# Two accumulator tiles in the second pass: which block of a unit lies in which one

## The chip, the cores and the metric

The kernel runs on one core of a Trainium2 chip. The metric is the device time of one execution in microseconds (us), lower is better; the median of a few runs is compared. One further execution was taken with the hardware profiler, and all rows below come from that one.

The engines are named as in the profile: PE is the matrix engine and PEld its weight loads, ACT the scalar engine, DVE the vector engine, POOL the general one, SP the one that issues most DMAs.

## The reference, cut to what matters

Two layers work on an image batch `x` of 8 x 96 x 96 pixels with 192 channels, float32 throughout. Layer 0 normalizes `x` by groups, projects it to 384 channels, convolves it 3 x 3, adds four running averages, normalizes each pixel over its 384 channels and projects back to 192. Layer 1 normalizes by groups, convolves 7 x 7, and has a two-layer network with a gelu per pixel. The change is in the part that ends layer 0:

```python
mu = jnp.mean(mixed, axis=-1, keepdims=True)
var = jnp.mean(jnp.square(mixed - mu), axis=-1, keepdims=True)
normed = (mixed - mu) * jax.lax.rsqrt(var + LN_EPS) * ln_g + ln_b
return jnp.einsum('bhwc,cd->bhwd', normed, W_out) + b_out   # then x + ...
```

## The kernel before, in words

The program is written in passes, one after the other, each with its own pools of buffers. The first pass (lines 245 to 570) is the group norm and the projection to 384 channels; it keeps its result in DRAM. The next (lines 605 to 827) is the 3 x 3 convolution with the running averages, and leaves `mixed` in DRAM as `M_d`, channels along the partitions. The pass of this change follows (lines 1045 to 1293; the change's own words call it the second pass). Last come the 7 x 7 convolution (`conv_d`, matmuls on line 1337) and the two-layer network (lines 1534 to 1595). Inside the pass the order on each engine is the order of the code: it stands under `manual_schedule`, and an engine's list of instructions is worked off strictly from the front.

**Units and blocks.** The pass goes over 192 units (`n_u`). A unit is one image column of four images, 384 pixels, and it has three blocks `j` of 128 pixels. For each block:

- `turn_c` (line 1135) transposes the 384 channels of the 128 pixels into a tile `pt`, three PE instructions.
- `project_c` (line 1141) multiplies the same pixels by the output weights `wc` and accumulates over three channel chunks `m` into a slot `po` of 193 columns. A float32 product is two PE instructions, so there are six. The last column of `wc` is 1/384, so column 193 of the slot is the pixel's mean.
- `square_c` (lines 1160 and 1162) runs on ACT: it copies the mean out of `po[:, D:]`, and then takes the sum of squares of `pt - mean` into column `j` of `var`.

One unit later, in this order: `scale_c` (lines 1168 and 1170) makes `rs` from `var`, first on DVE and then as a power on POOL; `finish_c` (line 1175) has DVE read the three slots `po`, j = 0, 1, 2 in turn, scale them by `rs`, add the input `xr` and write `x1c`. On DVE three statistics of `x1c` (line 1192) stand between the two in most units. On POOL the addition of a constant to the next `xr` (line 1261) follows the power.

**The accumulators.** `tile_po` takes two tiles of two slots each from a pool of four tiles (`ps_o`), each tile in a PSUM bank of its own. Three of the four slots are used. So the two tiles of a unit are handed out again two units later, and the first matmul into one of them then waits until `finish_c` has read all that lay in it. Waits are set by tile: a matmul into one slot of a tile also waits for an engine that still reads the other slot. `pt` has a pool of three tiles (`ps_t`), one a block.

**Loads and stores.** In the iteration of unit u, SP issues the loads of unit u+3 (`mt` in two parts of 384 and 192 KB, line 1111, and `xr` of 288 KB, line 1123), and, when a group of 16 units is complete, one of its twelve stores of 384 KB each (line 1211) in each of the next twelve units. `mt` has four buffers. In the last 36 units loads for the next pass are added (`raw` on line 926, on SP and POOL, and `band` on line 936). After unit 95 the group norm's sums over the first half are made, in five steps, one a unit (`norm_c`, lines 988 to 1043): DVE waits in them for small matmuls of PE.

**The start.** Because `M_d`'s last rows come late, the first two chunks (`range(NC - 1)`) of some blocks of units 0 and 1 are multiplied ahead of the loop (lines 1231 to 1233). `ms` on line 1265 says, for these two units, which chunks are left to each block.

Of the kernel before, what the change touches and what calls it, by code (L numbers as in the profile page):

```python
# [101 lines left out]
def conv_blocks_kernel(  # L102
# [36 lines left out]
    NC = C // 128  # L139
# [111 lines left out]
    with ExitStack() as ph:  # L251
# [258 lines left out]
        with tc.manual_schedule():  # L510
# [13 lines left out]
            for b in range(B):  # L524
                more = b + 1 < B
                for t in range(n_t):
                    u = b * n_t + t

                    n, j = divmod(u - 2, NJ)
# [25 lines left out]
                    k, j = divmod(t, NJ)  # L555
# [489 lines left out]
    with ExitStack() as ph:  # L1045
# [10 lines left out]
        NJ3 = 3  # L1056
# [4 lines left out]
        def make_wc(stores):  # L1061
            ps = ps_s.tile([128, 512], F32, tag="gn_ps", name="ps_w")
            nc.gpsimd.memset(wc[:, :, D:], 1.0 / C)
            for m in range(NC):
                nc.scalar.activation(
                    wc[:, m, :D], wo[:, m], AF.Identity, scale=gb[:, 0, m : m + 1]
                )
            for step in stores:
                step()
            for lo, lhs, rhs in ((D, lnb, wo), (0, None, wc)):  # L1070
                for m in range(NC):
                    nc.tensor.matmul(
                        ps[:, lo : lo + D],
                        mean_w if lhs is None else lhs[:, m],
                        rhs[:, m, :D],
                        start=(m == 0),
                        stop=(m == NC - 1),
                    )
            for m in range(NC):
                nc.vector.tensor_tensor(wc[:, m, :D], wc[:, m, :D], ps[:, :D], ALU.subtract)  # L1080
            nc.vector.tensor_tensor(cst, bo, ps[:, D : 2 * D], ALU.add)
            nc.gpsimd.memset(blk, 0.0)
            for b in range(NH):
                q = slice(b * QH, (b + 1) * QH)
                nc.gpsimd.memset(blk[q, q], 1.0 / QH)
                nc.gpsimd.tensor_copy(
                    pick[:, b], ident[:, b * QH : b * QH + 1].to_broadcast([128, 128])
                )
# [13 lines left out]
        def load_m(u, k):  # L1102

            hf, p, v = place_c(u)
            w = v * PH + p
            if u not in mts and u < 3:
                mts[u] = first[:, u].rearrange("p (m n) -> p m n", m=NC)
            elif u not in mts:
                mts[u] = ip.tile([128, NC, NH * S], F32, tag="mt", name="mt")
            m = (slice(0, CS // 128), slice(CS // 128, NC))[k]  # L1110
            nc.sync.dma_start(
                mts[u][:, m],
                M_f[k][S - 1 - w, :, hf * NH * S : (hf + 1) * NH * S].rearrange(
                    "(m c) n -> c m n", c=128
                ),
            )

        def load_x(u):

            hf, p, v = place_c(u)  # L1120
            w = v * PH + p
            xrs[u] = ip.tile([128, NJ3, D], F32, tag="xr", name="xr", bufs=5)
            nc.sync.dma_start(
                xrs[u],
                x_f[hf * NH * S : (hf + 1) * NH * S, w].rearrange("(i j) c -> i j c", j=NJ3),
            )

        def load_c(u):
            for k in range(2):
                load_m(u, k)  # L1130
            load_x(u)

        def turn_c(mt, pt, j, ms):
            for m in ms:
                nc.tensor.transpose(
                    pt[:, m * 128 : (m + 1) * 128], mt[:, m, j * 128 : (j + 1) * 128], ident
                )

        def project_c(mt, po, j, ms):
            for m in ms:  # L1140
                nc.tensor.matmul(  # L1141
                    po,
                    mt[:, m, j * 128 : (j + 1) * 128],
                    wc[:, m],
                    start=(m == 0),
                    stop=(m == NC - 1),
                )

        def tile_pt():
            return ps_t.tile([128, C], F32, tag="pt", name="pt")  # L1150

        def tile_po():
            pa = ps_o.tile([128, 2, D + 1], F32, tag="po", name="po")
            pb = ps_o.tile([128, 2, D + 1], F32, tag="po", name="po")
            return [pa[:, 0], pa[:, 1], pb[:, 0]]

        def square_c(pt, po, var, j):

# [60 lines left out]
        with tc.manual_schedule():  # L1219
            for u in range(3):  # L1220
                load_m(u, 0)
            make_wc(late_b)
            for u in range(3):
                load_m(u, 1)
            for u in range(3):
                load_x(u)
            pos_c = {u: tile_po() for u in range(2)}
            pts_c = {j: tile_pt() for j in range(NJ3)}
            for j in range(NJ3):
                turn_c(mts[0], pts_c[j], j, range(NC - 1))  # L1230
            for u in range(2):
                for j in range(0, NJ3, 2):
                    project_c(mts[u], pos_c[u][j], j, range(NC - 1))
            weights = load_weights()
            for u in range(n_u + 1):
                if weights and u >= 8:
                    with nc.allow_non_contiguous_dma(reason="one value per partition"):
                        nc.scalar.dma_start(*weights.pop(0))
                if u + 3 < n_u:
                    load_c(u + 3)  # L1240
                if stores:
                    stores.pop(0)()
                if u == n_u - 36:
                    early_d = [lambda: load_band(0)]
                    early_d += [lambda t=t: load_raw(0, t) for t in range(NT)]
                    early_d += [lambda: load_band(1)]
                if u >= n_u - 36 and u % 3 == 0 and early_d:
                    early_d.pop(0)()
                if u == n_u - 14:
                    first_d += scale_steps(0)  # L1250
                    for t in range(NT):
                        first_d.insert((t + 1) * 9 - 1, lambda t=t: load_raw(1, t))
                if u >= n_u - 14:
                    for step in first_d[:3]:
                        step()
                    del first_d[:3]
                if held is not None:
                    rs = scale_c(held[1])
                if u < n_u:
                    mt, xr = mts.pop(u), xrs.pop(u)  # L1260
                    nc.gpsimd.tensor_tensor(
                        xr, xr, cst.unsqueeze(1).to_broadcast([128, NJ3, D]), ALU.add
                    )
                    var = sp.tile([128, NJ3], F32, tag="var", name="var")
                    ms = [range(NC - 1 if u in pos_c and j != 1 else 0, NC) for j in range(NJ3)]
                    pos = pos_c.pop(u) if u in pos_c else tile_po()
                    for j in range(NJ3):
                        pt = pts_c.pop(j) if j in pts_c else tile_pt()
                        turn_c(mt, pt, j, range(0 if u else NC - 1, NC))
                        project_c(mt, pos[j], j, ms[j])  # L1270
                        square_c(pt, pos[j], var, j)
                if steps:
                    for step in steps.pop(0):
                        step()
                if held is not None:
                    n, v = divmod(u - 1, WQ)
                    if v == 0:
                        x1c = xps[1 - n % 2].tile([128, NJ3, D, WQ], F32, tag="x1c", name="x1c")
                    finish_c(x1c, v, held[0], rs, held[2])
                    if v == WQ - 1:  # L1280
                        steps += group_steps(x1c, n)
                        stores += [
                            lambda x=x1c, n=n, j=j, q=q: store_c(x, n, j, q)
                            for j in range(NJ3)
                            for q in range(NX)
                        ]
                held = (pos, var, xr) if u < n_u else None
            for step in first_d:
                step()
            for store in stores:  # L1290
                store()
            for step in sum(steps, []):
                step()

    WE = 8
    NJ3 = 3
# [487 lines left out]
```

## Time and profile before

| What | us |
|---|---|
| median of 3 runs (5494.1 to 5501.23) | 5495.28 |
| the profiled execution's own time | 5491.53 |
| its span, first to last instruction | 5489.7 |
| the pass of the change, from the span's start | 1803 to 2621 |
| PE busy over the span | 5298.0 (97%) |
| L1141, the pass's projections, on PE: 3456 instructions | 686.7 |
| L1135, its transposes, on PE: 1728 instructions | 283 |

How to read it: the time of an execution is some 2 us longer than its span. A row of the timeline gives start, duration, engine, line, operation, the tiles written and read, and the count; the brackets at the end give the idle time of the engine just before, and who ended it. Rows of PEld are the weight loads that go ahead of each matmul and run beside the one before.

### The profile page before, as it was taken

The numbers are of one execution on the slowest core, as the hardware profiler recorded it, in microseconds if no ns is written. First come the engines' busy times: TensorE is split into PE (matmuls) and PEld (weight loads), VectorE is DVE, ScalarE is ACT, GpSimd is POOL, SyncE is SP. The second block draws the span as 40 slices with busy tenths as digits, with TensorE's granted clock in tenths as the row PEclk, the third lists the DMA queues.
The fourth block names the chain that finished last, engine by engine and source line by source line (L and its number), as shares of the span: only waits on it lengthen the run. The fifth ranks groups of instructions, "written<-read, shape, count | busy, mean of one in ns | idle before, by whom it ended". The sixth has DMA issues, their size and how long they took to land. (4 is left out here: it accounts for less than half of the span.)

```text
span 5489.7 us, 108072 instructions
## 1 busy us (share of the span) xinstructions
PE 5298.0 (97%) x42206; PEld 3359.4 (61%) x42206; DVE 3450.2 (63%) x6706; ACT 2593.6 (47%) x5781; POOL 2366.2 (43%) x2063
## 2 busy tenths in 40 slices
PE   6999999999999999999787899999999999999999
PEld 4666643333333899899454566666666676666767
DVE  6556539999999455555556455555566666656654
ACT  2444447777777566566434444444433233333332
POOL 1211128888888555555322232322233333333332
PEclk9999979999999999999898999999999999999999
DMA  7999869999998899899996454555433233333231
GB/s 222 285 288 276 245 179 244 243 243 244 246 242 230 247 293 293 260 287 315 290 294 171 117 136 124 131 137 137 111 90 80 79 79 80 88 91 84 79 79 41
DMA packets 793486, 1015.35 MB, mean 185 GB/s; under 512 B 331191, under 2 KB 668320, under 8 KB 790928
## 3 DMA queue, kind: packets, MB, share of 16 engines
q1 hardware_dynamic: 677000, 634.43, 44.2%
q0 software_dynamic: 84304, 331.93, 18.2%
q10 hardware_dynamic: 31672, 42.08, 3.4%
q8 instruction: 333, 5.46, 0.4%
q14 instruction: 177, 1.45, 0.1%
HBM read 603.70 MB, written 420.03 MB: 186 GB/s over the span
## 5 line engine op out<-in xcount | busy, mean ns | idle before, releaser
L1574 PEld LDWEIGHTS hp<-w1g,g 128*128 128x128 f32 x6912 | 1117.9, 190 | 140.7 <-issue 75.8
L1574 PE MATMUL hp<-w1g,g 128*128 128x192 f32 x6912 | 1174.9, 329 | 0.0
L1563 ACT ACTIVATE g<-hp,b0g 128x512 f32<-128x512 f32 x864 | 520.2, 693 | 1211.3 <-PE hp L1554 1188.0
L1593 POOL DMA_DIRECT2D out_dram<-xo x288 | 211.6, 735 | 1574.4 <-DVE xo L1585 1480.7
L1585 DVE TENSOR_TENSOR xo<-hp,r 128x384 f32<-128x384 f32 x288 | 229.0, 795 | 992.9 <-PE hp L1574 987.9
L1544 PE MATMUL hp<-yT,w0w 128*128 128x512 f32 x1728 | 780.6, 598 | 20.3 <-DVE yT L1529 20.3
L1141 PE MATMUL po<-wc,mt 128*128 128x193 f32 x3456 | 686.7, 334 | 7.4 <-DVE x1c L1175 7.1
L688 PE MATMUL pl<-pin,band 34*32 34x380 f32 (+1 forms) x13824 | 640.2, 497 | 6.2 <-DMA pin<-PL_d 4.0
L775 POOL TENSOR_TENSOR mo<-mo,z 128x768 f32<-128x768 f32 x285 | 592.5, 2079 | 5.7 <-ACT mo L713 1.6
L1141 PEld LDWEIGHTS po<-wc,mt 128*128 128x128 f32 x3456 | 555.7, 191 | 39.4 <-ACT mean L1160 31.0
L1544 PEld LDWEIGHTS hp<-yT,w0w 128*128 128x128 f32 x1728 | 321.5, 191 | 380.9 <-issue 346.2
L721 DVE TENSOR_TENSOR_SCAN z<-decay,loc 128x768 f32<-128x768 f32 x288 | 506.0, 1757 | 64.7 <-ACT loc L697 36.3
L1337 PE MATMUL hp<-xin,band 63*64 63x372 f32 (+1 forms) x4608 | 422.8, 503 | 95.2 <-ACT yo L1347 35.6
L730 DVE TENSOR_TENSOR_SCAN z<-decay,z 128x768 f32<-128x768 f32 x288 | 498.5, 1731 | 0.1
L688 PEld LDWEIGHTS pl<-pin,band 34*32 34x32 f32 x13824 | 234.1, 108 | 394.1 <-issue 390.1
L1508 POOL TENSOR_TENSOR rs<-tot,neg_half 32x32 f32<-32x32 f32 x72 | 394.8, 5483 | 122.3 <-DVE tot L1506 121.0
L709 PE MATMUL pa<-loc,mix 128*32 128x384 f32 x3456 | 439.4, 500 | 0.0
L712 PE MATMUL pa<-last,down 96*32 96x384 f32 x1152 | 434.2, 500 | 1.0 <-ACT mo L713 1.0
L1554 PE MATMUL hp<-yT,w0w 64*128 64x512 f32 x1728 | 419.5, 611 | 0.0
L1347 ACT ACTIVATE yo<-hp,dwb 128x384 f32<-128x384 f32 x384 | 197.6, 585 | 435.6 <-PE hp L1337 272.8
L697 ACT COPY loc<-pl 128x384 f32<-128x384 f32 x576 | 248.6, 484 | 312.7 <-PE pl L688 312.7
L395 PE MATMUL pm<-xT,win 128*128 128x384 f32 x1152 | 391.7, 490 | 0.0
(155 smaller groups left out, 7248.1 us busy)
## 6 DMA issues: line engine op xcount, KB each, us to landing
P<-po POOLq DMA_DIRECT2D x96, 1152.0 KB, 9.5
pin<-P SPq DMA_DIRECT2D x190, 576.0 KB
mt<-M SPq DMA_DIRECT2D x192, 384.0 KB
xq<-in_x_dram SPq DMA_DIRECT2D x96, 576.0 KB
xr<-in_x_dram SPq DMA_DIRECT2D x192, 288.0 KB
X<-x1c SPq DMA_DIRECT2D x144, 384.0 KB
out_dram<-xo POOLq DMA_DIRECT2D x288, 192.0 KB, 2.5
r<-X SPq DMA_DIRECT2D x35, 1536.0 KB
```

The source lines that it names most:

```text
L688: nc.tensor.matmul(pls[g][at * RB : (at + 1) * RB, :, lo:hi], band[rows, c, kh, :], pin[rows, c, :, NJ - 1 - j, lo + kh - 1 : hi + kh - 1] ...
L709: nc.tensor.matmul(pa[at], mix[:, i, at], loc[:, q], start=True, stop=True)
L712: nc.tensor.matmul(pa[at], down[:, to], last[:, q], start=True, stop=True)
L721: nc.vector.tensor_tensor_scan(zf, decay_f, loc.rearrange("p q n -> p (q n)"), 0.0, ALU.mult, ALU.add)
L730: nc.vector.tensor_tensor_scan(zr, decay_f, zr, 0.0, ALU.mult, ALU.add)
L775: eng.tensor_tensor(m, m, z, ALU.add)
L1141: nc.tensor.matmul(po, mt[:, m, j * 128 : (j + 1) * 128], wc[:, m], start=(m == 0), stop=(m == NC - 1),)
L1337: nc.tensor.matmul(pys[g][k * 64 : (k + 1) * 64, :, lo:hi], band[rows, k * GS + c, d * ZS : d * ZS + 64], xin[rows, :, :, k * GS + c, lo + ...
L1544: nc.tensor.matmul(hps[m, q], w0w[:, 0, m * 128 : (m + 1) * 128], yT[:, 2 * q], start=True, stop=False,)
L1554: nc.tensor.matmul(hps[m, q], w0w[p, 1, m * 128 : (m + 1) * 128], yT[p, 1], start=False, stop=True,)
L1563: nc.scalar.activation(g[:, m, q], hps[m, q], AF.Gelu, bias=b0g[:, m : m + 1], scale=1.0)
L1574: nc.tensor.matmul(po[:, q], g[:, m, q, k * 128 : (k + 1) * 128], w1g[:, m], start=(m == 0), stop=(m == NE - 1),)
```

## The change

The second and the third block of a unit change slots: block 1 goes to the first slot of the second tile, and block 2 to the second slot of the first tile. What is multiplied ahead of the loop changes with it: blocks 0 and 1 of the first two units in place of blocks 0 and 2.

```diff
-            return [pa[:, 0], pa[:, 1], pb[:, 0]]
+            return [pa[:, 0], pb[:, 0], pa[:, 1]]
...
             for u in range(2):
-                for j in range(0, NJ3, 2):
+                for j in range(2):
                     project_c(mts[u], pos_c[u][j], j, range(NC - 1))
...
-                    ms = [range(NC - 1 if u in pos_c and j != 1 else 0, NC) for j in range(NJ3)]
+                    ms = [range(NC - 1 if u in pos_c and j < 2 else 0, NC) for j in range(NJ3)]
```

In the order of instructions, TensorE's list alone differs, in some ten rows of units 0 and 1; the number of instructions is the same on every engine. The waits differ: block 1's first projection waits for DVE as block 0's does, block 2's for ACT, and the first transpose of block 2 has two things to wait for (PE and ACT) where it had one (PE).

## The prediction

> **What bounds the kernel now.** I read the page first: PE is busy 97% of the span, so only what PE waits for in the pass of the change can be won. Of the page's groups these two are the projections of that pass. The columns after the bar are busy us, mean ns, and PE's idle time just before with who ended it.
>
> ```profile
> span 5489.7 us, 108072 instructions
> ...
> L1141 PE MATMUL po<-wc,mt 128*128 128x193 f32 x3456 | 686.7, 334 | 7.4 <-DVE x1c L1175 7.1
> ...
> L1141 PEld LDWEIGHTS po<-wc,mt 128*128 128x128 f32 x3456 | 555.7, 191 | 39.4 <-ACT mean L1160 31.0
> ```
>
> The matmuls themselves hardly wait (7.4 us), but their weight loads stood still 31.0 us for ACT's copy of the mean. Busy matmuls hide this: a PE row that began without its weights ready is only longer. The waits inside 1804 to 2621 give the count (total us, times, longest):
>
> ```profile
> PEld po L1141 <- ACT mean L1160: 31.0, 190, 0.5
> ...
> PEld pt L1135 <- DMA mt<-M: 8.5, 4, 7.9
> PEld po L1141 <- DVE x1c L1175: 8.1, 4, 3.6
> ```
>
> So once a unit, in 190 of 192 units. The timeline of one steady unit shows what such a wait costs. Block 0 begins at 2102.64, block 1 at 2103.95, block 2 at 2105.45, the next unit at 2106.77:
>
> ```profile
> 2102.64 0.49 PE L1135 MATMUL pt<-ident,mt 128*128 128x128 f32 x3
> ...
> 2102.97 1.15 PE L1141 MATMUL po<-wc,mt 128*128 128x193 f32 x6
> ...
> 2103.95 0.49 PE L1135 MATMUL pt<-ident,mt 128*128 128x128 f32 x3
> ...
> 2104.15 0.16 ACT L1160 COPY mean<-po 128x1 f32<-128x1 f32 x1 [0.45 <-PE po L1141]
> ...
> 2104.36 0.95 PEld L1141 LDWEIGHTS po<-wc,mt 128*128 128x128 f32 x6 [0.16 <-ACT mean L1160]
> 2104.36 1.25 PE L1141 MATMUL po<-wc,mt 128*128 128x193 f32 x6
> ...
> 2104.95 1.28 DVE L1175 SCALAR_TENSOR_TENSOR x1c<-po,rs,xr 128x192 f32<-128x192 f32 x3
> 2105.29 0.41 PEld L1135 LDWEIGHTS pt<-ident,mt 128*128 128x128 f32 x3
> 2105.45 0.49 PE L1135 MATMUL pt<-ident,mt 128*128 128x128 f32 x3
> ...
> 2106.77 0.49 PE L1135 MATMUL pt<-ident,mt 128*128 128x128 f32 x3
> ```
>
> ACT's copy of block 0's mean (2104.15, 0.16 long) ends at 2104.31, and block 1's projection, into the same tile, begins 0.05 later. Blocks 0 and 2 project 0.33 after their transposes, block 1 only 0.41 after; and its six matmuls take 1.25 and not 1.15, as no weights were ready. From start to start the blocks take 1.314, 1.501 and 1.314 (medians over 189 or 190 units): a wait costs **0.187 us**, and a unit 4.13.
>
> **The change part by part.**
>
> *The wait that goes.* Block 1 now writes the second tile, so it need not wait for ACT to read block 0's mean. Block 2 does instead (it shares the first tile with block 0), but it projects one block, over 1.3 us, after that copy ended; nothing is late there. The three blocks should all take 1.314: 190 x 0.187 = **-35.5 us**. If hidden weight loads alone were won it would be the 31.0 of the waits view; I take the spacing, which counts PE itself.
>
> *An added wait instruction.* Block 2's transposes now have two things to wait for. Such pairs stand in the trace as a separate 51 ns instruction of PE's sequencer, two a unit (382), ahead of blocks 0 and 1. Block 2 has none. The step from block 2 to block 0, which has one, is 1.314 like the one without: nothing, as the sequencer runs ahead of PE. Bounds 0 and 190 x 0.051 = 9.7; I take 0.
>
> *A later release.* Block 0 of unit u+2 takes the first tile again. That tile was free after `finish_c`'s reads of blocks 0 and 1; now it needs those of 0 and 2, the last of the three, some 0.4 later (1.28 for three). Behind this wait stands all of PE's list. In the unit shown the three reads end at 2106.23, and the weight load they must precede is at 2106.99. Over all units that gap is 0.73 to 0.75 at nearly every one; with a unit 0.187 shorter and 0.05 for the signal, **0.50 us is left**. So it costs nothing in the steady part. Where `norm_c` holds DVE up, it does:
>
> ```profile
> 2270.89 1.26 DVE L1175 SCALAR_TENSOR_TENSOR x1c<-po,rs,xr 128x192 f32<-128x192 f32 x3
> 2271.84 2.20 PE L1141 MATMUL po<-wc,mt 128*128 128x193 f32 x6 [3.32 <-DVE x1c L1175]
> ```
>
> PE starts 0.32 before the last of the three reads ends; now it will start 0.05 after. Four units are like this: 4 x 0.37 = **+1.5 us**.
>
> *What is late next: the DMAs.* A unit with a store moves 384 + 192 + 288 + 384 KB = 1.278 MB, 309 GB/s at 4.13 us; twelve of sixteen units have one, the others move 0.885 MB. At 3.94 us it is 324 GB/s in those twelve. To see the room, I counted the 1536-byte packets off against the issues of `mt`: up to unit 158 they are in 5 to 9 us ahead of their first transpose (least 2.6, at unit 64), of the three units' lead (12.4). Should the DMAs give no more than today's 309, twelve units lose 12 x 0.187 = 2.2 us of that room, and the four without a store give it back. So it is hidden. In the last 36 units it isn't (columns: us, busy of PE, PEld, DVE, ACT, POOL, clock, DMA share, GB/s):
>
> ```profile
> 1900.00:2000.00 100.00, 100.00 (x656) 94.47 (x655) 53.28 (x148) 60.41 (x218) 54.05 (x48) 1.00 0.95 298
> ...
> 2500.00:2540.00 40.00, 40.00 (x262) 37.55 (x261) 23.73 (x66) 24.04 (x88) 23.12 (x21) 1.00 1.08 335
> ...
> 2570.00:2612.00 42.00, 41.35 (x267) 38.30 (x265) 28.25 (x80) 24.83 (x90) 24.24 (x23) 1.00 1.08 310
> ```
>
> With the loads for the next pass the DMAs are full, and the room falls from 6.7 at unit 159 to 0.21 at unit 172, rises to 8.7 at 179, and falls to 0.13 at unit 190, after PE had already waited 1.1 us in two blocks (one row: 0.47 for `mt` at 2603.15). If the DMAs are no faster, a shorter unit takes 0.56 (three units' lead) and 0.187 a unit from this. At unit 172: 0.21 - 0.56 - 13 x 0.187 = -2.8. At unit 190: 0.13 - 1.1 - 0.56 - 8 x 0.187 = -3.0, of which 1.1 is paid today. So **+2.8 and +1.9, together +4.7 us**. Bounds: 0 (the DMAs can give more), and the whole gain of these 36 units, 6.7.
> The Trainium skill weighs on this: its page "DMA: Bandwidth & Descriptors", in "Where 436 GB/s comes from", gives some 358 GB/s as one core's share of the memory. By it the 335 above had room left, the tail would cost nothing, and the time would be some 5 us lower. The rows of the trace, a share of 1.08 with the room shrinking, speak against it.
>
> *The start.* Four pairs of chunks are multiplied ahead of the loop as before, only for other blocks. PE waits there for `mt` (7.6 and 7.9 us), so this costs nothing, with 0.3 either way.
>
> *What follows.* The next pass begins with `finish_c` of the last unit: the last twelve stores go out from 2623.47, behind them on SP's queue the next `band`, and PE waits 21.2 us for that. All of it hangs on the end of this pass and moves with it. Between 2621 and 3070 the clock flips often, which may add or take a few us.
>
> **Sum:** -35.5 + 1.5 + 4.7 = -29.3. The profiled execution would go from 5491.53 to 5462.2; the median shown is 3.75 above it, so 5495.28 - 29.3 = **5466**.
>
> **The rivals.**
>
> *The DMAs bind all through the pass.* Then the units with a store stay at 4.13 and only four of sixteen gain: 35.5 / 4 = 9 us, 5486. For it: a share of 0.95 already. Against: 5 us of room and 335 GB/s where asked for. Chance 0.08.
>
> *The time of block 1 isn't the wait's.* If PE needs the 0.187 for changing tiles, nothing moves: 5495. Against: blocks 0 and 2 also change tiles (block 2 to the second, block 0 to the next unit's) without it. Chance 0.03.
>
> *Slower: the later release becomes the bound.* From the last projection of a unit (ends 2102.80) over ACT, `ve`, `rs` and three reads to the release (2106.28) takes 3.48 us, and there is one unit for it, 3.94. It decides from 3.94 on, and beyond 4.13 the pass is slower than now: `rs` on POOL (0.86) or a statistic on DVE would have to take 0.65 more. The 0.42 of one read, paid in each of 190 units, is 80 us against 35.5: 5540. Against: the gap is the same to 0.02 us in nearly all units. Chance 0.03.
>
> *The clock.* After the 3.32 us stall above PE ran at half clock (2.20 for six matmuls in place of 1.25), which cost 1.7 us in the rows that follow. If the two DMA stalls of the tail and one longer stall of `norm_c` do that, and some of the flips after 2621 fall badly, it is 5 to 9 us: 5473. Chance 0.06.
> The Trainium skill's "TensorE: Matmul & The Clock Gate", under "A second HAM failure mode: psum-queue depth-cycling", tells of small idle times from cycling through PSUM banks that drop the clock over and over. The trace doesn't bear that out: four tiles are cycled through here now, at a granted clock of 1.00.
>
> **How the numbers follow.** The forecast has 0.80. A change under 0.2%, 11 us, can't be told from none. Faster: 0.80 + 0.06 + half of the first rival 0.04 = 0.90; same: 0.04 + 0.03 = 0.07; slower 0.03. The range's low end is -35.5 with no cost of `norm_c` or tail and 3 us for the runs' spread: 5457. Its high end takes in 9.7 for the wait instruction, or the clock with a dearer tail: 5481. What is left out is most of the first rival, no effect, and slower.
>
> **What would show it.** Right: no wait of L1141's weight loads for ACT's mean, blocks of 1.31 all three, a steady unit of 3.94, mean PE time of L1141 near 329 ns; the four waits for `x1c` longer by 0.4 each; waits for `mt` of about 3 us near units 172 and 190, and the next pass some 29 us earlier. Wrong: waits for `x1c` in many units, a third wait row in each unit with a gap behind it, or units of 4.1 with waits for `mt`.

## The result, and the profile after

The changed kernel took 5463.48 us (median of 6 runs, 5442.51 to 5470.07), the kernel before 5494.4 beside it (6 runs, 5479.02 to 5501.23): a ratio of **0.995**, interval 0.9933 to 0.9967. On a second chip it was 5464.61 (10 runs) against 5487.31 (15 runs), ratio 0.9957 (0.9943 to 0.9971). 5466 was forecast. The profiled execution took 5470.07 us, its span is 5468.3, so it is 21.4 shorter in span than that of before.

The page after, the two groups of the pass's projections:

```profile
L1141 PE MATMUL po<-wc,mt 128*128 128x193 f32 x3456 | 668.8, 329 | 7.4 <-DVE x1c L1175 7.3
...
L1141 PEld LDWEIGHTS po<-wc,mt 128*128 128x128 f32 x3456 | 557.7, 192 | 9.0 <-DVE x1c L1175 8.6
```

The weight loads' wait for ACT's mean is gone from its place in the second row (39.4 us of idle time before, 9.0 now), and the matmuls, though as many, are 17.9 us less busy: those of the second block are no longer stretched. The timeline of a steady unit after, from block 0 to block 0:

```profile
2100.45 0.49 PE L1135 MATMUL pt<-ident,mt 128*128 128x128 f32 x3
...
2101.77 0.49 PE L1135 MATMUL pt<-ident,mt 128*128 128x128 f32 x3
2101.97 0.16 ACT L1160 COPY mean<-po 128x1 f32<-128x1 f32 x1 [0.45 <-PE po L1141]
2101.99 0.96 PEld L1141 LDWEIGHTS po<-wc,mt 128*128 128x128 f32 x6
2102.09 1.15 PE L1141 MATMUL po<-wc,mt 128*128 128x193 f32 x6
...
2103.08 0.49 PE L1135 MATMUL pt<-ident,mt 128*128 128x128 f32 x3
...
2104.39 0.49 PE L1135 MATMUL pt<-ident,mt 128*128 128x128 f32 x3
```

The blocks are 1.31 apart throughout. ACT copies a mean from 2101.97 to 2102.13, and PE's next projection begins within that time, at 2102.09; before, it stood 0.05 behind the copy's end.

The gain did not last to the end of the pass. These are PE's waits for `mt` from 2400 to the pass's end (total us, times, longest), first after, then before:

```profile
PE pt L1135 <- DMA mt<-M: 7.5, 7, 3.6
```

```profile
PE pt L1135 <- DMA mt<-M: 0.5, 1, 0.5
```

So I split the pass by the first transposes of its units in each trace, for all kernels (us; the last column is from the pass's first transpose to the first matmul of the 7 x 7 convolution):

| Kernel | steady unit | units 2-109 | 109-115 (`norm_c`) | 115-159 | 159-191 (extra loads) | whole pass |
|---|---|---|---|---|---|---|
| before | 4.131 | 442.1 | 37.1 | 181.7 | 133.9 | 817.4 |
| changed | 3.944 | 422.3 | 36.6 | 173.5 | 138.6 | 792.9 |
| changed, second profile | 3.944 | 422.3 | 36.5 | 173.5 | 136.9 | 791.1 |
| changed, loads moved | 3.944 | 422.0 | 34.9 | 175.6 | 127.0 | 781.7 |
| before, loads moved | 4.129 | 441.8 | 35.6 | 182.3 | 132.1 | 814.9 |
| blocks 1 and 2 share | 4.130 | 441.9 | 35.7 | 181.7 | 135.9 | 818.8 |
| a tile for each block | 5.302 | 567.7 | 42.5 | 233.3 | 169.8 | 1039.0 |
| changed, block 1 read first | 3.944 | 422.3 | 33.8 | 173.5 | 135.8 | 787.5 |
| both: loads moved, block 1 first | 3.944 | 421.9 | 33.8 | 175.0 | 127.7 | 780.1 |

In the profiled executions the pass gained 24.5 us. Another 2.3 had been gained before it began, and 5.4 were lost after it, where nothing was changed. Most of these were lost in the first 380 us behind the pass, where the mean granted clock was 0.86 and not the 0.87 of before; what brought that about is open. The column 109-115 holds a difference that was in no kernel's plan: behind its waits the granted clock fell to half for 3.4 us, twice in the first three rows, and once only in the rows with the loads moved or block 1 read first. One such stretch is worth some 1.6 us there.

### The profile page after: what moved, and what is told of

Read it like the earlier page. It is cut to its first block, busy times and chain, and to the rows that moved or that the text cites. A ratio compares the mean times of both kernels' runs of the same rounds, so it can differ in the third digit from the quotient of the medians.

```text
span 5468.3 us, 108263 instructions
## 1 busy us (share of the span) xinstructions
PE 5262.7 (96%) x42206; PEld 3344.9 (61%) x42206; DVE 3451.2 (63%) x6706; ACT 2588.0 (47%) x5781; POOL 2364.3 (43%) x2063
## 5 line engine op out<-in xcount | busy, mean ns | idle before, releaser
L1544 PE MATMUL hp<-yT,w0w 128*128 128x512 f32 x1728 | 780.1, 597 | 20.8 <-DVE yT L1529 20.8
L1141 PE MATMUL po<-wc,mt 128*128 128x193 f32 x3456 | 668.8, 329 | 7.4 <-DVE x1c L1175 7.3
L1337 PE MATMUL hp<-xin,band 63*64 63x372 f32 (+1 forms) x4608 | 423.3, 504 | 100.0 <-ACT yo L1347 39.4
```

What stands on the lines that cost most here:

```text
L1141: nc.tensor.matmul(po, mt[:, m, j * 128 : (j + 1) * 128], wc[:, m], start=(m == 0), stop=(m == NC - 1),)
L1337: nc.tensor.matmul(pys[g][k * 64 : (k + 1) * 64, :, lo:hi], band[rows, k * GS + c, d * ZS : d * ZS + 64], xin[rows, :, :, k * GS + c, lo + ...
L1544: nc.tensor.matmul(hps[m, q], w0w[:, 0, m * 128 : (m + 1) * 128], yT[:, 2 * q], start=True, stop=False,)
```

## The experiments

Theory: the wait for ACT's copy cost 0.187 us a unit, it is gone, and from unit 159 on the DMAs take back what a shorter unit wins. Rivals: block 1 was slow for another reason (its slot, a change of tile); the late release of the first tile, or the clock, is what slows the tail.

**Blocks 1 and 2 share.** Block 0 has the first tile alone:

```diff
-            return [pa[:, 0], pb[:, 0], pa[:, 1]]
+            return [pa[:, 0], pb[:, 0], pb[:, 1]]
```

> Block 0 alone in the first tile, blocks 1 and 2 in the two slots of the second. Theory: the wait for ACT's copy of the mean comes back, now in front of block 2 (for block 1's mean), 190 times, blocks of 1.31, 1.31 and 1.50, a unit of 4.13, the time that of before within 3 us (5490 to 5497). The first tile is free after one read, so the stalls where the group norm holds DVE up get 0.4 shorter each. Rival (block 1 was slow for lying in the second slot or for the change of tile, not for the wait): no long block, or another one than block 2, and 5463.

Measured: 5491.2 us (10 runs) against 5487.88 for the kernel before on the same chip, ratio 1.0011 (1.0001 to 1.0021). The timeline of blocks 1 and 2 of one unit:

```profile
2106.16 0.49 PE L1135 MATMUL pt<-ident,mt 128*128 128x128 f32 x3
...
2106.49 1.15 PE L1141 MATMUL po<-wc,mt 128*128 128x193 f32 x6
...
2107.48 0.49 PE L1135 MATMUL pt<-ident,mt 128*128 128x128 f32 x3
...
2107.89 0.95 PEld L1141 LDWEIGHTS po<-wc,mt 128*128 128x128 f32 x6 [0.16 <-ACT mean L1160]
2107.89 1.25 PE L1141 MATMUL po<-wc,mt 128*128 128x193 f32 x6
...
2108.98 0.49 PE L1135 MATMUL pt<-ident,mt 128*128 128x128 f32 x3
```

Block 1 (2106.16) now takes 1.32, and block 2 (2107.48), which follows its neighbour into the same tile, 1.50, with the same 0.16 before its weight load. The wait goes where the sharing neighbours go, and all of the gain goes with it. The rival is out: the second slot alone costs nothing, as block 2 of the changed kernel lies in one and takes 1.314, and a change of tile costs nothing, as block 1 here makes one. The waits for `x1c` where the group norm holds DVE up came to 6.0 us in place of 7.1: three of the four are 0.36 shorter, near the foretold 0.4, and one is as long as before.

**A tile for each block.** Three of the four tiles a unit, so that nothing is shared but a tile comes back after four blocks. What is multiplied ahead of the loop is cut to unit 0, and DVE's steps for the norm stand behind `finish_c`:

```diff
-            pa = ps_o.tile([128, 2, D + 1], F32, tag="po", name="po")
-            pb = ps_o.tile([128, 2, D + 1], F32, tag="po", name="po")
-            return [pa[:, 0], pb[:, 0], pa[:, 1]]
+            ps = [ps_o.tile([128, 2, D + 1], F32, tag="po", name="po") for _ in range(NJ3)]
+            return [p[:, 0] for p in ps]
```

> Each block in a tile of its own, from the same four tiles, so that no tile is shared but each comes back after four blocks, not six; the two things DVE does between power and reads stand behind the reads. Theory: what decides is the release: block 1 must wait for DVE's first read of the unit before, which ends some 2.6 us after that unit's last projection, where 1.6 us are there; a unit takes 4.8 to 5.1, the time 5620 to 5700, with waits of L1141 for x1c in all units. Rival (sharing is all that counts): 3.94 a unit and 5463.

Measured: 5704.02 us (one run), a unit 5.302. PE's waits and the row of one unit:

```profile
PE po L1141 <- DVE x1c L1174: 214.2, 191, 5.5
```

```profile
2106.73 1.29 DVE L1174 SCALAR_TENSOR_TENSOR x1c<-po,rs,xr 128x192 f32<-128x192 f32 x3 [1.04 <-POOL rs L1169]
...
2107.32 1.25 PE L1141 MATMUL po<-wc,mt 128*128 128x193 f32 x6 [1.09 <-DVE x1c L1174]
```

Once a unit, PE stands until DVE has read block 0 of the unit before. 5.302 - 3.944 = 1.36 us a unit, where I had reckoned about 1.0, and the time lies just beyond the 5620 to 5700 given. This is what the slower rival of the forecast described, a release that comes too late: sharing a tile with the neighbour costs 0.187 a unit, and needing a tile back two blocks sooner 1.36.

**The extra loads moved.** The `band` and `raw` loads of the next pass go into units 125 to 157, most of them without stores, and the second `raw` group starts eight units earlier:

```diff
-                if u == n_u - 36:
+                if u == n_u - 67:
...
-                if u >= n_u - 36 and u % 3 == 0 and early_d:
+                if u >= n_u - 67 and u % 16 in (13, 15) and early_d:
...
-                if u == n_u - 14:
+                if u == n_u - 22:
...
-                if u >= n_u - 14:
+                if u >= n_u - 22:
```

> The changed kernel, with the extra loads for the next pass (two band, six raw) moved from the last 36 units into earlier units, mostly those without stores. Theory: near the end the changed kernel waits for mt because the DMAs are full there (units 159 to 191 took 138.6 us, where 32 x 3.944 = 126.2 would do); with the loads moved these waits nearly vanish, units 159 to 191 take 127 to 131 us, and the time is 8 to 12 us below the profiled changed kernel, some 5452 to 5458. Rival (the late release of the first tile, or the clock, makes the tail slow): the tail keeps its 138, and the time stays at 5463 or above.

> The same move of loads in the kernel before. Theory: there the tail lost only 1.7 us (133.9 for 32 x 4.131 = 132.2), so the move is worth 0 to 2 us, ratio 0.999 to 1.001. Rival: if the move helps by itself and not because the units are shorter, it wins 8 to 12 us here too.

Measured in the changed kernel: 5451.47 us (4 runs) against 5487.88 for the kernel before, ratio 0.994 (0.9925 to 0.9956). By this alone it can't be told from the changed kernel (0.9933 to 0.9967); the pass shows the difference. Units 159 to 191 take 127.0 us. Of PE's waits for `mt` after 2400 this is left:

```profile
PE pt L1135 <- DMA mt<-M: 0.4, 1, 0.4
```

In the kernel before the same move gave 5480.21 (10 runs), ratio 0.999 (0.9978 to 1.0001). The medians are 7.7 us apart, which looks like the rival's 8 to 12; but of the 15.8 us between the two profiled executions only 2.5 lie in the pass. Its units 159 to 191 take 132.1 in place of 133.9, 1.7 us, of which 115-159 gives 0.6 back. In the changed kernel it is 138.6 or 136.9 to 127.0, of which 115-159 gives 2.1 back. So where these loads stand costs the longer unit 1 us and the shorter one 8 to 10. That tells for the DMAs, and against the release, which the move doesn't touch. The clock had a part, but as a consequence, and in one of the two profiles only: after the longest wait for `mt` (3.6 us, at 2484.06) a projection took 2.14 us in place of 1.15. In the second profile the granted clock was 1.00 through the tail, and it still took 136.9.

**Block 1 read first.** DVE's reads in `finish_c` take another order; the reason stands in the next section.

```diff
-            for j in range(NJ3):
+            for j in (1, 0, 2):
                 nc.vector.scalar_tensor_tensor(
```

> The changed kernel, with DVE reading block 1 first, then 0 and 2. New theory: the pool hands the tile that is read out first to the next unit's first tile, so block 0 now waits only for one read in place of two: the four waits for x1c where the group norm holds DVE up come to about 6.0 us in place of 7.3, each PE start 0.05 after the first read's end; nothing else moves. The theory of the prediction (block 0 waits for the tile of blocks 0 and 2): still the last read, 8.4 to 8.8.

Measured: 5449.38 us (one run), PE's waits for `x1c` on line 1141 (first row) and one of the four places:

```profile
PE po L1141 <- DVE x1c L1175: 6.2, 4, 3.0
```

```profile
2237.88 1.27 DVE L1175 SCALAR_TENSOR_TENSOR x1c<-po,rs,xr 128x192 f32<-128x192 f32 x3
2238.46 0.96 PEld L1141 LDWEIGHTS po<-wc,mt 128*128 128x128 f32 x6 [3.19 <-DVE x1c L1175]
```

The waits fall from 7.3 to 6.2: PE goes on 0.58 after the start of the three reads, where it was 0.95. The new theory foretold 6.0; the prediction's would have them grow. Three of the four waits are 0.37 shorter. The third is as long as before (2.25), as PE comes to it that much sooner. Units 109 to 115 take 33.8 in place of 36.5, but 1.6 of these 2.7 us are the clock's: only one stretch at half clock follows the waits here, and two did in both profiles of the changed kernel. Beside the changed kernel with the loads moved, which reads in the old order and has one stretch too, it is 34.9 to 33.8: the 1.1 us of the waits.

**The changed kernel again, and both improvements together**, on one chip. The second kernel has the moved loads, the second group two units earlier still (`n_u - 24`), and block 1 read first.

> The changed kernel once more, for its time beside the next one on the same chip and for a second profile of its tail. Theory: units of 3.944 again, and units 159 to 191 in 133 to 140 us (DMA-bound, the amount differs by execution), 0.995 of before.

> The changed kernel with both: the extra loads moved into earlier units (the second group two units earlier than in the run that moved them before), and DVE reading block 1 first. Theory: units 159 to 191 take 126 to 127.5 us, no wait for mt in the tail, and the time is 8 to 13 us below the changed kernel of the same chip, 0.992 to 0.994 of before. Rival (the gain of the moved loads was another chip's): the same as the changed kernel.

Measured: 5464.61 (10 runs) for the changed kernel, ratio 0.9957 (0.9943 to 0.9971), and **5442.65** (6 runs) for both together, ratio 0.9928 (0.991 to 0.9945), the best of the study. The medians are 22 us apart, more than the 8 to 13 foretold. Of the 25.3 us between the two profiled executions the pass won 791.1 - 780.1 = 11.0, some 1.6 of it by one stretch at half clock less in the units 109 to 115; 14.1 lie ahead of the pass, where nothing was changed, and the last section shows the clock there. Units 159 to 191 took 127.7, just over the 126 to 127.5 given, with one wait for `mt` of 0.2 left.

## Why the prediction was right, and where not

- *The wait that goes*: right, to the nanosecond that the trace gives. A unit went from 4.131 to 3.944. Units 2 to 109 and 115 to 159, 151 of the 190, won 19.8 + 8.2 = 28.0 us, and 151 x 0.187 is 28.2. That it goes with the neighbours is shown by the run that puts it before block 2.
- *An added wait instruction*: it is there (573 in place of 382) and costs nothing, as taken; the blocks it stands before are 1.314 apart.
- *A later release*: the step failed in its mechanism. I had block 0 wait for the tile of blocks 0 and 2. In the trace after, PE starts 0.05 after the second read's end and 0.32 before the third's, just as before; the waits are 7.3 us in place of 7.1, not 8.6. One of the four places in the trace after:

```profile
2248.07 1.26 DVE L1175 SCALAR_TENSOR_TENSOR x1c<-po,rs,xr 128x192 f32<-128x192 f32 x3
2249.02 1.34 PEld L1141 LDWEIGHTS po<-wc,mt 128*128 128x128 f32 x6 [3.55 <-DVE x1c L1175]
2249.02 1.85 PE L1141 MATMUL po<-wc,mt 128*128 128x193 f32 x6 [3.32 <-DVE x1c L1175]
```

  So what block 0 waits for is the read of block 1, second in this order, and when that read was put first, PE started 0.05 after the first. What fits both is that the pool hands out first the tile that is free first: block 1's tile is read out before that of blocks 0 and 2, so block 0 of the unit after next gets block 1's old one, and the two tiles change places. The traces don't name the banks, so this order is inferred from the two orders of reading. Reading block 1 first, which by my step would change nothing or lose, let PE go on one read sooner in each of the four places. The +1.5 was 0.2 in waits, all of it at the third place, where PE with its shorter units came 0.18 sooner to a release that stayed where it was. Units 109 to 115 got 0.5 shorter where full blocks would have made it 1.1.
- *The tail*: the mechanism was right, the size not. I forecast that units 159 to 191 would win 6.0 by the shorter unit and lose 4.7. They lost 10.7 (133.9 to 138.6), and 9.0 in the second profile: past the 6.7 that I had called the bound. That bound said that the tail could at worst be as slow as before, and it got slower. Two things are in it. After the 3.6 us wait the clock dropped for one stretch, 1.7 us over three blocks; the second profile has no such stretch. And the DMAs gave less. These are the windows in which `mt` of units 159 to 172 came in, before, after and in the second profile (clock, DMA share and GB/s at the end):

```profile
2476.00:2536.00 60.00, 60.00 (x394) 56.71 (x393) 33.02 (x91) 36.50 (x131) 35.37 (x33) 1.00 1.08 312
```

```profile
2446.00:2510.00 64.00, 59.43 (x388) 56.63 (x386) 32.51 (x91) 36.09 (x131) 34.31 (x32) 0.97 1.08 286
```

```profile
2452.00:2516.00 64.00, 58.67 (x392) 55.48 (x391) 32.88 (x93) 36.58 (x132) 35.22 (x33) 1.00 1.07 293
```

  All are full by the share, but it is 286 and 293 GB/s in place of 312; packets of 768 bytes took 43 ns on average in the second window where they took 38 in the first. Over the whole tail the difference is smaller: 307 and 310 GB/s in place of 314. What makes the DMAs slower is open: no run here changed the mix of loads and stores without moving it. The 358 GB/s of the Trainium skill's page "DMA: Bandwidth & Descriptors" ("Where 436 GB/s comes from") were not reached in these windows; a sum by it, with no cost in the tail, would have been too low by all of the 9 to 11 us.
- *The start and what follows*: the start won 0.6 us where 0.3 either way was given. The next pass began 26.8 us earlier, where some 29 were foretold, and its first 380 us were 4.6 longer, within what was left open.
- *The sum*: -29.3 against -30.9 and -22.7 in the medians of the two chips, and -24.5 and -26.3 in the pass of the two profiles. It held because the tail's error, 4 to 6 us, is small beside the executions' spread (the six runs of the changed kernel span 28 us), not because each term did; that the first chip's medians came within 2 us of it is luck.

## What to carry to other kernels

A wait of 0.16 us before a weight load doesn't show as idle time of the matmuls (7.4 us in all here). It shows in the row of the weight loads (39.4 us), and with its whole price in the spacing of equal blocks, where one in three is longer; there it can be read and multiplied. When an engine gets faster in a stage that is fed by DMA, follow the lead of the loads unit by unit to the end of the stage: the place with the least of it takes the gain back, and can take back more than was won there. To say which wait a reused buffer brings, look in the trace at which read the first writer really waits for; here it followed the tile that was freed first, not the order in which the code asks for them.

## What the runs showed of the hardware

The stretches at half clock at the start of an earlier pass go with a large part of the spread. The second profile of the changed kernel and that of both improvements, in the first 100 us of the 3 x 3 convolution, where the code is the same (clock, DMA share, GB/s at the end):

```profile
750.00:850.00 100.00, 93.70 (x1122) 28.61 (x1120) 58.23 (x38) 43.71 (x103) 42.32 (x49) 0.66 0.70 173
```

```profile
750.00:850.00 100.00, 90.30 (x1376) 32.55 (x1378) 71.89 (x46) 52.93 (x127) 54.61 (x61) 0.86 0.78 210
```

With a clock of 0.66 PE did 1122 matmuls in them, with 0.86 it did 1376; the pass of the change then began at 1807.0 and 1792.9, 14 us apart. In the six traces with a single half-clock stretch there, its length and the start of the pass of the change go together, from 34.1 us and 1790.6 to 68.3 us and 1807.0. The ten times of the changed kernel on the second chip fall into two groups, 5450 to 5454 at a mean granted clock of 0.984 to 0.985 and 5468 to 5473 at 0.981 to 0.983, with one at 5461 (0.984). The Trainium skill's "TensorE: Matmul & The Clock Gate", under "What's actually happening", has the full clock back after about one busy window of 3.4 us; here, in the second profile of the changed kernel, PE was 94% busy from 757 to 825 at a granted clock of 0.50, and in the nine traces the half clock there lasted 27 to 68 us, in one stretch or two. For a change of half a per cent the pass must be compared with the pass, and the whole only over many executions.
